# Weights and statistics of the next stage, loaded and made inside the scan loop

## The chip, the core and the metric

The kernel runs on one core of a Trainium2 chip. The time is that of the device for one execution of the whole program, in microseconds (us); of several executions the median is given. One more execution was recorded by the hardware profiler, and the views of the profile come from it. The engines are named as the profile names them: PE (matrix products) with PEld (its weight loads), DVE (VectorE), ACT (ScalarE), POOL (GpSimd) and SP (SyncE, which issues every DMA of this kernel).

## What is computed

The model has four layers over 4 images of 64 x 64 positions with 96 channels. Layers 0 and 1 are state-space blocks with a scan in four directions; layers 2 and 3 work on tokens and are not touched by the change. Of a scan layer, cut to what matters (layer 0; layer 1 is alike):

```python
x = x + _L0_conv_ref(_gn(x), ...)        # _gn: group normalisation over an image
xz = einsum('bhwc,ec->bhwe', x, in_proj_w)           # 96 -> 2 x 192
xx, z = split(xz, 2);  z = silu(z)
xc = silu(conv_3x3_depthwise(xx) + conv_b)
xs = [xc, xc transposed, xc reversed, xc transposed and reversed]   # K = 4 directions
dts, B, C = split(einsum('bkdl,kcd->bkcl', xs, x_proj_weight), [6, 22])
delta = softplus(einsum('bkrl,kdr->bkdl', dts, dt_projs_weight) + dt_projs_bias)
h = exp(delta * A) * h + delta * B * u      # for each of 4096 positions, 192 channels, 16 states
y = sum over states of h * C
y = layernorm(sum of the four directions) * ln_gamma + ln_beta
out = einsum('bhwe,ce->bhwc', y * z, out_proj_w)
```

The group normalisation needs the mean and the variance of every group over a whole image before the first product with `in_proj_w` can be right.

## The kernel before, in words

**Phases.** The two scan layers are worked in four phases: layer 0 for image pair 0, layer 0 for pair 1, layer 1 for pair 0, layer 1 for pair 1. `run` (L708) does, for each phase p, first the preparation of p with the finish of phase p-1 beside it, then the scan loop of p. After the last scan loop comes the finish of the last phase, and then the token layers.

**Preparation** (`prepare`, L151). It opens the pools `prep` and `steps`, loads the weights x_proj, dt_w, conv_b and Ds (L174), sums Ds (`dsum`, L182), and then makes the statistics of the two images: eight tiles `raw` of 96 x 8 x 2 x 64 numbers are loaded through two buffers (L190), and a bn_stats on DVE takes each half of each tile (L192). From these, for each of the two images, bn_aggr (L196), two small products with the group matrix (L198, L205) and an inverse root make `gs`, mean and scale of each channel. The loads of in_w and conv_w (L211, L174) follow. Then come the convolution (`convolve`, L231, which reads each image again in tiles `rawi`, L252, for the product L258) and the steps that make delta, delta times u, B and C and store them to DRAM (`steps`, L293).

**Finish** (`finish`, L555). It loads four weights, in_w (the half for z), out_w, gam and bet (L560 to L566), then for each quarter of the image loads `ud_f` and `yk` (L580, L590), undoes the directions on PE, and makes normalisation, gate, output product and residual. `run` advances it by one piece whenever the sum of `beside` over the preparation's pieces reaches 1. `beside` is 0 until the statistics and `gs` are made, so no piece of the finish is taken before that.

**Scan loop** (`scan_phase`, L478). It runs over 128 units: 8 chunks of 512 positions (NC), and in each 16 blocks (NEB) of 12 channels (EB). Its order is written out by hand (`manual_schedule`); outside the loop a scheduler orders the instructions of each engine. A unit `at` has 12 places n = 0 to 11. At each place PE replicates delta four places ahead (L424), ACT makes the decay three ahead (L428), DVE scans (L435), PE contracts the unit before (L453) and ACT evicts its result (L465); at every third place POOL multiplies h by B (L418), half a unit ahead. At n = 11 SP's work is issued in this order: the four y stores of the unit before (L473), the load of b for the next chunk after block 8 and of c after block 15 (L355), and the loads of unit at+3: dlt (L386) and six h loads (L408), two of 768 KB and four of 384 KB. The tiles: h has 4 buffers, dlt and d 3, the others 2. Every engine takes its instructions in the order of the program, SP too.

**DRAM layout of the input.** x and the result of the first layer lie as [pair, channel, 64, image, 64]. A `raw` tile of both images is therefore one run of 4096 bytes per channel; a tile of one image is 8 runs of 256 bytes.

Of the kernel before, what the change touches and what calls it, by code (L numbers as in the profile page):

```python
# [22 lines left out]
C = 96  # L23
E = 192
# [97 lines left out]
class Phase:  # L122


    def __init__(self, pre, pair, x_in, x_out):
        self.pre, self.pair, self.x_in, self.x_out = pre, pair, x_in, x_out

        self.beside = 0.0


class Scans:
    def __init__(self, tc, ctx, cst, a):
        nc = self.nc = tc.nc
        self.tc, self.cst, self.a = tc, cst, a

        def pool(name, bufs, **space):
            return ctx.enter_context(tc.tile_pool(name=name, bufs=bufs, **space))

        self.dram = pool("stage", 2, space=DRAM)
        self.keep = pool("keep", 2)  # L140
        cst.scans(tc, pool("const_s", 1))

    def bank(self):
# [7 lines left out]
    def prepare(self, ph):  # L151

        nc, cst, a, pre = self.nc, self.cst, self.a, ph.pre
        ph.gs = self.keep.tile([C, 2, 2], F32, name="gs", bufs=3)
        ph.delta = [
            self.dram.tile([G, NP16, E, TC], BF16, name="delta", bufs=2 * NC) for _ in range(NC)
        ]


        ph.du = [  # L160
            self.dram.tile([2, G, E + PITCH, TC], F32, name="du", bufs=2 * NC) for _ in range(NC)
        ]
        ph.bc = [self.dram.tile([NS // 2, G, 4, TC], F32, name="bc", bufs=2 * NC) for _ in range(NC)]
        ph.ud = self.dram.tile([C, 2, HW, 2, 64], F32, name="ud")
        ph.y = self.dram.tile([64, G, 2, 2, NEB, 16 * EB], F32, name="y")
        x = ph.x_in[ph.pair]

        with self.tc.tile_pool(name="prep", bufs=1) as wp, self.tc.tile_pool(
            name="steps", bufs=2
        ) as sp:  # L170

            def load(name, shape, at=0):
                t = wp.tile([at + shape[0]] + shape[1:], F32, name=name)
                nc.sync.dma_start(t[at:], a[pre + name])  # L174
                return t

            xp = load("x_proj", [C, 2, 2, XD2])
            dt_w = load("dt_w", [XD2 - 2 * NS, 2, E], at=2 * NS)
            conv_b = load("conv_b", [C, 2])
            ds = load("Ds", [C, 2, K])  # L180
            dsum = wp.tile([C, 2], F32, name="dsum")
            nc.vector.tensor_reduce(dsum, ds, mybir.AxisListType.X, ALU.add)  # L182
            yield


            st = wp.tile([C, 2, 8, 6], F32, name="st")
            with self.tc.tile_pool(name="stats", bufs=2) as rp:
                for hl in range(8):
                    raw = rp.tile([C, 8, 2, 64], F32, name="raw")
                    nc.sync.dma_start(raw, x[:, hl * 8 : hl * 8 + 8])  # L190
                    for i in range(2):
                        nc.vector.bn_stats(st[:, i, hl], raw[:, :, i])  # L192
                    yield
            for i in range(2):
                mv = wp.tile([C, 2], F32, name="mv")
                nc.vector.bn_aggr(mv, st[:, i].rearrange("p c s -> p (c s)"))  # L196
# [12 lines left out]
                yield  # L209
            in_w = wp.tile([C, E], F32, name="in_w")  # L210
            nc.sync.dma_start(in_w, a[pre + "in_proj_w"][:, :E])  # L211
            taps = load("conv_w", [C, 2, 9])

            xc = [wp.tile([C, 2, L], F32, name="xc", bufs=2) for _ in range(2)]
            ph.beside = 1.0
            yield
            yield from self.convolve(ph, 0, x, xc[0], in_w, taps, conv_b, dsum)
            ph.beside = 0.6
            other = self.convolve(ph, 1, x, xc[1], in_w, taps, conv_b, dsum)
            for i in range(2):  # L220
# [8 lines left out]
                ph.beside = 1.25  # L229

    def convolve(self, ph, i, x, xc, in_w, taps, conv_b, dsum):  # L231

# [242 lines left out]
                u.d[t::4, t].rearrange("p h l x -> p h (l x)"),  # L475
            )

    def scan_phase(self, ph):  # L478

# [16 lines left out]
        with self.tc.tile_pool(name="units", bufs=2) as self.units, self.tc.tile_pool(  # L496
            name="p_a", bufs=6, space=PSUM
        ) as self.p_a, self.tc.tile_pool(name="p_y", bufs=2, space=PSUM) as self.p_y:
            with self.tc.manual_schedule():
# [12 lines left out]
                    ahead(t, self.replicate)  # L512
                for t in range(LEAD - 1):
                    ahead(t, self.decay)
                for at, u in enumerate(units):
                    before = units[at - 1] if at else None
                    for n in range(EB):
                        t = at * EB + n
                        ahead(t + LEAD, self.replicate)
                        ahead(t + LEAD - 1, self.decay)  # L520
                        self.scan(u, n)
                        q, part = divmod(n, 3)
                        if before:
# [12 lines left out]
                        if n == 7 and u.eb >= NEB - 2 and u.c + 1 < NC:  # L536
                            self.weights(ph, u.c + 1, u.eb)
                        if n == EB - 1:
                            if before:
                                self.store(before)  # L540
                            if u.eb == 8 and u.c + 1 < NC:
                                self.load_b(ph, u.c + 1)
                            if u.eb == NEB - 1 and u.c + 2 < NC:
                                self.load_c(ph, u.c + 2)
                            if at + 3 < last:
                                self.load(units[at + 3])
# [8 lines left out]
    def finish(self, ph):  # L555
        nc, cst, a, pre = self.nc, self.cst, self.a, ph.pre
        x, x_out = ph.x_in[ph.pair], ph.x_out[ph.pair]
        with self.tc.tile_pool(name="fin", bufs=1) as fp:
            in_w = fp.tile([C, E], F32, name="in_w")
            nc.sync.dma_start(in_w, a[pre + "in_proj_w"][:, E:])  # L560
            out_w = fp.tile([C, 2, C], F32, name="out_w")
            nc.sync.dma_start(out_w, a[pre + "out_proj_w"])
            gam = fp.tile([128, E], F32, name="gam")
            nc.sync.dma_start(gam, a[pre + "gamma"].broadcast_to([128, E]))
            bet = fp.tile([128, E], F32, name="bet")
            nc.sync.dma_start(bet, a[pre + "beta"].broadcast_to([128, E]))  # L566
# [141 lines left out]
    def run(self, phases):  # L708


        for p in range(len(phases) + 1):
            with self.tc.tile_pool(name="p_c", bufs=2, space=PSUM) as self.p_c, self.tc.tile_pool(
                name="p_d", bufs=2, space=PSUM
# [9 lines left out]
                for _ in end:  # L723
                    pass
            if p < len(phases):
                self.scan_phase(phases[p])


@with_exitstack
# [268 lines left out]
```

## Time and profile before

| | |
|---|---|
| median of 3 runs | 11881.9 us (11853.94 to 11897.37) |
| the profiled execution | 11923.01 us, its span 11921.2 us |
| busy in the span | PE 72%, DVE 84%, ACT 62%, POOL 63% |
| chain that ended last | DMA 57%, PE 12%, DVE 11%, SP's queue 10% |
| DMA | 2501 MB, 210 GB/s over the span |
| mean granted PE clock | 0.827 |

By stages, cut at the first and last scan of each phase (busy us of the engines and GB/s of the DMA in the stage):

| stage | us | PE | DVE | ACT | POOL | GB/s |
|---|---|---|---|---|---|---|
| preparation 0 | 723.3 | 327.9 | 446.5 | 336.8 | 117.5 | 162 |
| scan loop 0 | 1870.7 | 1437.6 | 1806.5 | 1279.7 | 1741.9 | 250 |
| finish 0, preparation 1 | 847.2 | 538.0 | 551.2 | 431.7 | 122.9 | 183 |
| scan loop 1 | 1861.3 | 1434.2 | 1805.3 | 1276.4 | 1741.8 | 251 |
| finish 1, preparation 2 | 847.1 | 528.7 | 551.2 | 431.7 | 121.5 | 183 |
| scan loop 2 | 1860.3 | 1435.4 | 1805.0 | 1277.7 | 1742.9 | 251 |
| finish 2, preparation 3 | 850.8 | 540.8 | 551.2 | 432.1 | 120.9 | 182 |
| scan loop 3 | 1857.4 | 1436.1 | 1804.5 | 1276.5 | 1743.0 | 251 |
| finish 3 | 337.9 | 239.1 | 105.0 | 87.1 | 0.0 | 114 |
| token layers | 865.2 | 632.2 | 565.5 | 505.3 | 27.8 | 16 |

The shares over the span mix stages with different limits, so the stage is what to read. In a line of the profile that tells of a group of instructions, the text has the engine, the source line, the operation, and the tiles as out<-in with partitions x elements; after the bar or in brackets stands the idle time of that engine just before, and what ended it. "SPq" is SP's queue: an issue of a DMA, not the transfer.

### The profile page before, as it was taken

How to read it: one execution, taken by the hardware profiler on the slowest of the kernel's cores; microseconds unless marked ns; L12 is line 12 of the kernel's file. 1: busy time of each engine (PE TensorE's matmuls, PEld its weight loads, DVE VectorE, ACT ScalarE, POOL GpSimd, SP SyncE). 2: the span in 40 equal slices, each digit the busy share in tenths (PEclk: the TensorE clock that was granted, in tenths of full speed). 3: DMA queues.
4: the chain of work that ended last, by engine and by line, in shares of the span. 5: the costliest groups of instructions: out<-in, count | busy, mean ns of one | idle time of the engine just before them, and what ended most of it. 6: DMA issues, size and time to landing. Idle time of an engine off the chain costs nothing.

```text
span 11921.2 us, 337611 instructions
## 1 busy us (share of the span) xinstructions
PE 8549.8 (72%) x144992; PEld 4586.7 (38%) x144992; DVE 9991.8 (84%) x10247; ACT 7335.1 (62%) x12106; POOL 7480.2 (63%) x2316
## 2 busy tenths in 40 slices
PE   4557777765767777765767777766667777777777
PEld 1124444432334444442334444433234444444333
DVE  6679999977779999987769999986769999993667
ACT  4556666655556666655556666655557666662556
POOL 0169999961159999970149999980149999980000
PEclk8578999986679999986679999887578898998887
DMA  3677777765677777765777777765677777763110
GB/s 99 192 244 250 253 255 254 251 208 144 201 241 256 253 253 251 253 217 146 204 229 258 256 253 251 253 217 149 198 226 255 255 255 253 253 229 124 18 22 11
DMA packets 952266, 2501.22 MB, mean 210 GB/s; under 512 B 324494, under 2 KB 607220, under 8 KB 819316
## 3 DMA queue, kind: packets, MB, share of 16 engines
q1 hardware_dynamic: 950772, 2479.63, 63.0%
q8 instruction: 1142, 18.71, 0.7%
q14 instruction: 352, 2.88, 0.1%
HBM read 1965.42 MB, written 513.80 MB: 208 GB/s over the span
## 4 chain that ended last, share of the span: by engine, by line
DMA 57%; PE 12%; DVE 11%; SPq 10%; ACT 5%; issue 3%; POOL 2%; POOLq 0%; DVEq 0%; ACTq 0%
DMA h<-du 53%; SPq L408 9%; DVE xc L277 4%; PE f L603 2%; POOL parts L331 2%; PE d L317 1%; DVE dl L328 1%; PE f L683 1%; PE c L300 1%; DVE du_sb L327 1%; PE f L694 1%; DVE parts L332 1%; DMA yk<-y 1%; PE f L669 1%; PE f L612 1%
## 5 line engine op out<-in xcount | busy, mean ns | idle before, releaser
L418 POOL TENSOR_TENSOR h<-h,b 128x1536 f32<-128x1536 f32 x2048 | 7020.9, 3461 | 574.0 <-DMA h<-du 229.6
L435 DVE TENSOR_TENSOR_SCAN h<-a,carry,h 128x512 f32<-128x512 f32 x5376 | 6353.3, 1259 | 202.8 <-POOL h L418 199.4
L428 ACT ACTIVATE a<-a,a_col 128x512 f32<-128x512 f32 x6144 | 4038.5, 664 | 1888.6 <-PE a L424 1852.8
L453 PEld LDWEIGHTS y<-h,cw 128*32 128x32 f32 x131072 | 2785.0, 128 | 3534.2 <-issue 1369.4
L453 PE MATMUL y<-h,cw 128*32 128x48 f32 x131072 | 3658.4, 266 | 522.4 <-DVE h L435 205.3
L424 PE MATMUL a<-dlt,rep 72*128 72x512 bf16 x6144 | 2534.2, 422 | 1352.5 <-DVE h L435 1254.1
L331 POOL CAST parts<-dl 96x1024 bf16<-96x1024 f32 x256 | 431.2, 1688 | 2687.6 <-DVE dl L328 1979.4
L465 ACT COPY d<-y 128x384 f32<-128x384 f32 x2048 | 979.7, 478 | 467.7 <-PE y L453 414.9
L435 DVE TENSOR_TENSOR_SCAN h<-a,h 128x512 f32<-128x512 f32 x768 | 868.2, 1200 | 179.7 <-ACT a L428 113.4
L277 DVE SCALAR_TENSOR_TENSOR xc<-xp,conv_w,xc 96x512 f32<-96x512 f32 x1024 | 716.3, 760 | 154.2 <-ACT xc L275 110.0
L424 PEld LDWEIGHTS <-rep 72*128 72x128 bf16 x6144 | 487.5, 98 | 849.3 <-issue 613.9
L317 PE MATMUL d<-xd,dt_w 7*96 7x512 f32 x1024 | 532.0, 885 | 263.6 <-ACT dl L325 141.2
L835 POOL MEMSET tn<- 1x4096 f32 x8 | 27.8, 3506 | 861.5 <-PE pa L855 515.4
L300 PE MATMUL c<-xc,x_proj 96*103 96x512 f32 x512 | 442.0, 1002 | 115.7 <-ACT xp L261 54.6
L327 DVE TENSOR_TENSOR du_sb<-dl,xc 96x1024 f32<-96x1024 f32 x256 | 409.9, 1607 | 123.6 <-ACT dl L325 67.2
L603 PE MATMUL f<-yk,perm 128*128 128x384 f32 x1024 | 415.6, 549 | 106.4 <-DMA yk<-y 81.0
L325 ACT ACTIVATE dl<-d 96x1024 f32<-96x1024 f32 x256 | 257.7, 1018 | 348.6 <-DVE parts L332 259.2
L328 DVE TENSOR_TENSOR dl<-dl,parts 96x1024 f32<-96x1024 f32 x256 | 309.8, 1216 | 190.7 <-ACT parts L326 187.8
L332 DVE TENSOR_TENSOR parts<-dl,parts 96x1024 bf16<-96x1024 f32 x256 | 326.2, 1280 | 170.0 <-POOL parts L331 168.8
L317 PEld LDWEIGHTS d<-xd,dt_w 7*96 7x96 f32 x1024 | 160.0, 216 | 586.5 <-ACT xd L303 200.1
L258 PE MATMUL c<-rawi,in_ws 96*96 96x512 f32 x256 | 195.5, 874 | 241.3 <-ACT xp L261 101.6
L370 ACT ACTIVATE cw<-c,gmask 128x256 f32<-128x256 f32 x512 | 285.5, 569 | 129.3 <-DMA dlt<-delta 66.7
(119 smaller groups left out, 5764.0 us busy)
## 6 DMA issues: line engine op xcount, KB each, us to landing
h<-du SPq DMA_DIRECT2D x1024, 768.0 KB
h<-du SPq DMA_DIRECT2D x2048, 384.0 KB
du<-du_sb SPq DMA_DIRECT2D x512, 384.0 KB
delta<-parts SPq DMA_DIRECT2D x256, 576.0 KB
dlt<-delta SPq DMA_DIRECT2D x512, 288.0 KB
y<-d SPq DMA_DIRECT2D x2048, 48.0 KB
yk<-y SPq DMA_DIRECT2D x256, 384.0 KB
ud<-xu SPq DMA_DIRECT2D x128, 192.0 KB
```

The source lines that it names most:

```text
L277: nc.vector.scalar_tensor_tensor(rows(acc), src, w, rows(acc), ALU.mult, ALU.add)
L300: nc.tensor.matmul(rows(ps[:XD2]), xp[:, k, h], u[:, h], start=h == 0, stop=h == 1)
L317: nc.tensor.matmul(ps[:, m], dt_w[part, k, m * C : (m + 1) * C], xd[part], start=True, stop=True)
L331: nc.gpsimd.tensor_copy(parts[:, 1], delta)
L408: self.nc.sync.dma_start(u.h[32 * first : 32 * (first + quarters), e : e + n].rearrange("p e t -> p (e t)"), source.rearrange("a g e t -> ...
L418: self.nc.gpsimd.tensor_tensor(h, h, b, ALU.mult)
L424: self.nc.tensor.matmul(u.a[n], self.cst.rep[:, h], u.dl[:, e], start=True, stop=True)
L428: self.nc.scalar.activation(u.a[n], u.a[n], AF.Exp, scale=u.ph.a_col[:, at : at + 1])
L435: self.nc.vector.tensor_tensor_scan(u.h[:, n], u.a.pop(n), u.h[:, n], 0.0 if u.c == 0 else u.ph.carry[:, at : at + 1], ALU.mult, ALU.add,)
L453: self.nc.tensor.matmul(view(u.y[32 * j : 32 * j + 32], l2 * EB, (8 * EB, 4), (1, EB)), u.ph.cw[u.c][:, l1, 8 * j + l2], view(u.h, 64 * l1 ...
L465: self.nc.scalar.copy(u.d[:, :, :, l1], u.y[:, : 32 * EB].rearrange("p (t h x) -> p t h x", t=4, h=2))
L603: nc.tensor.matmul(ps[:, : 4 * C].rearrange("p (w v e) -> p w v e", w=4, v=nv), cst.perm[:, k], view(t, off, (sw if k < 2 else -sw, 4), (1 ...
```

## The change

A new pool `weights` holds the ten weights of finish and preparation, one buffer each. A phase's preparation no longer loads its six weights; `prepare_weights` makes a list of six small tasks of it. For phase 0 `run` calls them at the start. The finish no longer loads its four; `finish_weights` makes four tasks of it. `statistics` makes 17 tasks: task n reduces tile n-1 and loads tile n, a tile now being one image's 96 x 8 x 64 numbers (16 tiles of 192 KB instead of 8 of 384 KB). In the scan loop, from unit 32 on, place 8 of each unit takes the next task of the list: the four weights of this phase's finish, then the six of the next preparation, then the 17 of its statistics, 27 in all (4 in the last loop). The loop's `raw` tile has the two buffers of the loop's pool. The preparation of phase 0 has no loop before it and runs the 17 tasks itself.

```diff
@@ prepare
-            xp = load("x_proj", [C, 2, 2, XD2])
-            dt_w = load("dt_w", [XD2 - 2 * NS, 2, E], at=2 * NS)
-            conv_b = load("conv_b", [C, 2])
-            ds = load("Ds", [C, 2, K])
+            xp, dt_w, conv_b, ds, in_w, taps = ph.prep_w
...
-            st = wp.tile([C, 2, 8, 6], F32, name="st")
-            with self.tc.tile_pool(name="stats", bufs=2) as rp:
-                for hl in range(8):
-                    raw = rp.tile([C, 8, 2, 64], F32, name="raw")
-                    nc.sync.dma_start(raw, x[:, hl * 8 : hl * 8 + 8])
-                    for i in range(2):
-                        nc.vector.bn_stats(st[:, i, hl], raw[:, :, i])
-                    yield
+            if ph.st is None:
+                with self.tc.tile_pool(name="stats", bufs=2) as rp:
+                    for part in self.statistics(ph, rp):
+                        part()
+                        yield
+            st = ph.st
...
-            in_w = wp.tile([C, E], F32, name="in_w")
-            nc.sync.dma_start(in_w, a[pre + "in_proj_w"][:, :E])
-            taps = load("conv_w", [C, 2, 9])
@@ new
+    def weight(self, name, shape, source, at=0):
+        t = self.wts.tile([at + shape[0]] + shape[1:], F32, name=name)
+        self.nc.sync.dma_start(t[at:], source)
+        return t
...
+    def prepare_weights(self, ph):
...
+        return [
+            lambda: load("x_proj", [C, 2, 2, XD2]),
+            lambda: load("dt_w", [XD2 - 2 * NS, 2, E], 2 * NS),
+            lambda: load("conv_b", [C, 2]),
+            lambda: load("Ds", [C, 2, K]),
+            load_in,
+            lambda: load("conv_w", [C, 2, 9]),
+        ]
...
+    def statistics(self, ph, pool):
...
+        ph.st = self.keep.tile([C, 2, 8, 6], F32, name="st")
...
+            raw = pool.tile([C, 8, 64], F32, name="raw")
+            nc.sync.dma_start(raw, x[:, hl * 8 : hl * 8 + 8, i])
...
+            nc.vector.bn_stats(ph.st[:, i, hl], loaded.pop(0).rearrange("c a p -> c (a p)"))
...
+            def part(n=n):
+                if n:
+                    reduce(*at[n - 1])
+                if n < len(at):
+                    load(*at[n])
@@ scan_phase(self, ph, after)
+                side = self.finish_weights(ph)
+                if after:
+                    side += self.prepare_weights(after)
+                    side += self.statistics(after, self.units)
+                side = iter(side)
...
+                        if n == 8 and at >= 2 * NEB:
+                            part = next(side, None)
+                            if part:
+                                part()
@@ finish
-            in_w = fp.tile([C, E], F32, name="in_w")
-            nc.sync.dma_start(in_w, a[pre + "in_proj_w"][:, E:])
...
+            in_w, out_w, gam, bet = ph.fin_w
@@ run
+        for part in self.prepare_weights(phases[0]):
+            part()
...
-                self.scan_phase(phases[p])
+                self.scan_phase(phases[p], phases[p + 1] if p + 1 < len(phases) else None)
```

More of the change, by code (lines that the diff above doesn't have):

```diff
@@ L128, in __init__ @@
         self.beside = 0.0
+        self.st = None
 class Scans:
@@ L140, in __init__ @@
         self.keep = pool("keep", 2)
+        self.wts = pool("weights", 1)
         cst.scans(tc, pool("const_s", 1))
@@ L170, in prepare @@
         ) as sp:
[L172 to L175, printed above, removed]
-            xp = load("x_proj", [C, 2, 2, XD2])
-            dt_w = load("dt_w", [XD2 - 2 * NS, 2, E], at=2 * NS)
-            conv_b = load("conv_b", [C, 2])
-            ds = load("Ds", [C, 2, K])
+            xp, dt_w, conv_b, ds, in_w, taps = ph.prep_w
             dsum = wp.tile([C, 2], F32, name="dsum")
@@ L229, in prepare, with load, load_in, finish_weights @@
                 ph.beside = 1.25
+    def weight(self, name, shape, source, at=0):
[3 more added lines that the diff above has]
+    def prepare_weights(self, ph):
+        def load(name, shape, at=0):
+            ph.prep_w.append(self.weight(name, shape, self.a[ph.pre + name], at))
+        def load_in():
+            ph.prep_w.append(self.weight("in_w", [C, E], self.a[ph.pre + "in_proj_w"][:, :E]))
+        ph.prep_w = []
+        return [
[6 more added lines that the diff above has]
+        ]
+    def finish_weights(self, ph):
+        a, pre = self.a, ph.pre
+        ph.fin_w = []
+        return [
+            lambda: ph.fin_w.append(self.weight("z_w", [C, E], a[pre + "in_proj_w"][:, E:])),
+            lambda: ph.fin_w.append(self.weight("out_w", [C, 2, C], a[pre + "out_proj_w"])),
+            lambda: ph.fin_w.append(
+                self.weight("gam", [128, E], a[pre + "gamma"].broadcast_to([128, E]))
+            ),
+            lambda: ph.fin_w.append(
+                self.weight("bet", [128, E], a[pre + "beta"].broadcast_to([128, E]))
+            ),
+        ]
+    def statistics(self, ph, pool):
+        nc, x = self.nc, ph.x_in[ph.pair]
+        ph.st = self.keep.tile([C, 2, 8, 6], F32, name="st")
+        loaded = []
+        def load(hl, i):
+            raw = pool.tile([C, 8, 64], F32, name="raw")
+            nc.sync.dma_start(raw, x[:, hl * 8 : hl * 8 + 8, i])
+            loaded.append(raw)
+        def reduce(hl, i):
+            nc.vector.bn_stats(ph.st[:, i, hl], loaded.pop(0).rearrange("c a p -> c (a p)"))
+        at = [(hl, i) for hl in range(8) for i in range(2)]
+        for n in range(len(at) + 1):
+            def part(n=n):
[3 more added lines that the diff above has]
+                    load(*at[n])
+            yield part
     def convolve(self, ph, i, x, xc, in_w, taps, conv_b, dsum):
@@ L476, in store, with scan_phase @@
             )
-    def scan_phase(self, ph):
+    def scan_phase(self, ph, after):
         nc = self.nc
@@ L558, in finish @@
         with self.tc.tile_pool(name="fin", bufs=1) as fp:
-            in_w = fp.tile([C, E], F32, name="in_w")
-            nc.sync.dma_start(in_w, a[pre + "in_proj_w"][:, E:])
[L561 to L566, printed above, removed]
+            in_w, out_w, gam, bet = ph.fin_w
             for q in range(4):
```

## The prediction

> **What bounds the kernel now.** I read the busy times in ten windows first, cut at the first and last scan (L435) of each phase. The four scan loops take 1870.7, 1861.3, 1860.3 and 1857.4 us, the preparations between them 847 to 851. A border has two edges, so both were looked at.
>
> In the loop VectorE is busy 97% of the time and GpSimd 93%, but neither sets the pace. The timelines of the two engines (start, length, line; in brackets the idle time before it) and then the chain of waits:
>
> ```profile
> 1217.40 14.21 DVE L435 TENSOR_TENSOR_SCAN h<-a,carry,h 128x512 f32<-128x512 f32 x12 [0.91 <-POOL h L418]
> 1232.47 14.21 DVE L435 TENSOR_TENSOR_SCAN h<-a,carry,h 128x512 f32<-128x512 f32 x12 [0.86 <-POOL h L418]
> ...
> 1213.92 13.69 POOL L418 TENSOR_TENSOR h<-h,b 128x1536 f32<-128x1536 f32 x4 [1.41 <-DMA h<-du]
> ```
>
> ```profile
> 1511.69 12.98 DMA h<-du
> 1524.68 0.02 issue
> 1524.69 0.69 SPq L408
> ```
>
> A unit is 12 scans, 14.2 us of VectorE and 13.7 us of GpSimd, yet units come every 14.6 us (scan start to scan start, mean after the eighth unit). VectorE waits 0.46 to 0.51 us at its first scan for GpSimd, and GpSimd 0.9 us at its first product for the DMA. The chain then stays in one loop: an h load lands, SP issues the next, that one lands. SP's issues use eight completion semaphores in turn, so an issue waits for the DMA eight places before it. The transfers set the pace, and VectorE has about 0.4 us a unit to spare.
>
> The DMA packet records say what saturates. For 97% of a scan loop at least 8 packets are in work on the 16 engines, for 27% exactly 8. An h load of 768 KB makes 16 semaphore updates, one of 384 KB makes 9, of which the first comes at once: the four small ones of each unit run on 8 engines. Those eight are nearly full, the other eight are not.
>
> At the border to the second phase (timeline):
>
> ```profile
> 2604.64 0.35 SPq L174 DMA_DIRECT2D x_proj<-in_L_x_proj  x1
> 2605.05 0.27 SPq L174 DMA_DIRECT2D dt_w<-in_L_dt_w  x1
> ...
> 2613.64 0.16 DVE L182 TENSOR_REDUCE dsum<-Ds 96x2 f32<-96x8 f32 x1 [19.50 <-DMA Ds<-in_L_Ds]
> 2613.86 2.47 DVE L192 BATCH_NORM_STATS2 st<-raw 96x6 f32<-96x512 f32 x4
> ...
> 2631.46 0.35 DVE L196 BATCH_NORM_AGGREGATE mv<-st 96x2 f32<-96x48 f32 x1
> ...
> 2640.98 3.73 PE L258 MATMUL c<-rawi,in_ws 96*96 96x512 f32 x4 [1.83 <-DVE ln L118]
> ```
>
> The last scan ended at 2594.0. SP waits until 2604.6 for the landing of the last y store, only then loads weights, and eight raw tiles go through two buffers. Nothing else runs: the convolution needs the statistics, and the finish begins beside it.
>
> **Gain at the borders.** From that first load (x_proj) to the first bn_aggr: 2604.64 to 2631.46, 5313.34 to 5340.84, 8020.57 to 8047.42: 26.8, 27.5 and 26.85 us. All of it goes, except the wait on the same landing and dsum, about 0.5 us: 26.3 + 27.0 + 26.35 = **79.7 us**. What is late next is the chain from bn_aggr to L258, 9.5 us, unchanged. L258's first two tiles are already there: of the 32 rawi loads (L252) of a phase, the first phase's stretch holds 34, the last two at 375.6 and 377.3 us. The finish's ud_f and yk loads, issued in 1.8 + 5.2 us, can start at 2604.7 and are in before the PE gets to them some 12 us later; without that cover a wait of up to 5 us a border appears. The last finish loses its four weight issues, 10728.84 to 10730.92: **2.1 us**.
>
> **Loss in the first phase.** It has no loop before it, so it still makes its statistics, now with 16 loads of 192 KB and one reduction behind each, where there were 8 of 384 KB. The nearest row is the rawi load, same shape: issued 41.84, used by the PE at 44.55, so 2.7 us. Two buffers then give two loads per 2.7 + 0.7 + 0.1 = 3.5 us; 14 after the first pair are 24.5 us, ending near 39 where it now ends at 31.7: **-7.5 us** (5 to 13).
>
> **Cost in the loop.** Per phase 0 to 2: 4 weights of the finish in units 32 to 35, 6 of the preparation in 36 to 41, 16 raw loads in 42 to 57 and 16 reductions in 43 to 58. Each is one more issue on SP (0.3 to 0.4 us), one more place in the ring of eight, and packets on the full engines.
>
> VectorE: a bn_stats is 0.67 us, issue to issue 0.61. A unit then needs at least 14.1 + 0.68 = 14.8 us against 14.6, so at least 0.2 us a unit if nothing else changes.
>
> The wait for raw: in program order it stands behind the h loads of the unit before and ahead of the y stores. SP gets there about 2 us into the next unit. The y stores issued there land 12.9 to 14.0 us into it (semaphore records, three units), so raw lands near 14. The reduction stands behind scan 8 of that unit, which ends at 10.66. VectorE stops there for about 3.4 us, with three scans of this unit and all of the next queued behind, and PE and ScalarE with them. I take that as paid once, not sixteen times: VectorE then runs 3.5 us later against a DMA stream that doesn't wait for it, and raw lands as VectorE arrives. How far it may lag is seen in one unit: its last eviction (L465) ended at 1522.94, its y store was issued at 1527.58, so 4.6 us. After unit 58 the 0.5 us that VectorE waits per unit pays the lag back in some 8 units.
>
> What is not paid back is time of the full engines. The nearest rows: rawi's 768 packets of 256 B occupied all 16 engines 1.04 to 1.29 us, so 1.0 to 1.1 us an engine. The trace holds a trial of an added load: b and c (256 KB, 128 packets), one each per 16 units between the y stores and dlt. Folding the issue times of dlt over units 16 to 111 of all phases: 14.6 in a usual unit, 16.16 then 13.11 around c, 16.82 then 12.87 around b. The pairs exceed 29.2 by 0.07 and 0.49 us. So one more load and one more place in the ring cost 0.1 to 0.5 us. Sixteen in a row can't use a neighbour's slack: from below 0.2 (VectorE's floor), from above 1.1 (every packet). I take about 1.0 less the 3% of idle time (0.44 us), 0.55: 16 x 0.55 = **8.8 us a phase** (3 to 18).
>
> The weights: nine are 0.1 to 0.6 us an engine, inside the idle share, 0.3 us together. dt_w is different. By its bytes, 106 KB at the loop's 250 GB/s, it costs 0.4 us. In the trace its 71 packets went out from 2606.28 to 2612.30, 6.0 us, while the loads around it had finished on 15 engines by 2611.8 and got their last update at 2613 to 2615. The Trainium skill (DMA: Bandwidth & Descriptors, "Why a DMA increments its semaphore by 16 and not by 1") says that the number of engines is the largest one up to 16 that divides the slowest dimension of both sides, and that these are the lowest-numbered. 71 is prime, so one engine, and that one is among the eight that the 384 KB loads (slowest dimension 8) use. It speaks against moving this load into the loop. By the bytes the phase costs 9.5 us, by the rule up to 15; I take the rule's side, 5 us after some idle time: **14 us a phase**, 42 in three. Which engine a packet ran on isn't in the records.
>
> **Sum.** 79.7 + 2.1 - 7.5 - 42 = 32 us faster. The profiled execution took 11,923.0 (span 11,921.2 and 1.8 around it), so 11,891 there. It lay 41 us above the median of three, 11,881.9; from the median, **11,850 us**. Those three spread 43 us; below 0.5% (59 us) I count as no change.
>
> **Rivals.**
> 1. The loop takes it all in: VectorE's floor and nothing more, about 3 us a phase. For it: b and c cost next to nothing. Against: each of these has two light units behind it. 79.7 + 2.1 - 7.5 - 9 = 65 faster, 11,817.
> 2. Slower: the stop for raw recurs in every unit. Place: the reduction behind scan 8. Price: 3.4 us x 16 x 3 = 163, with 3 x 5 for dt_w. It decides once VectorE's lag passes the 4.6 us: then the y stores wait for the evictions, the h loads and the next raw behind them move back too, and lag makes lag. Against: the first stop and the reduction make 4.1 us. 163 + 15 - 74 = 104 slower, 11,986.
> 3. The border gives less: the finish's yk loads, which now meet the last y store, or another order of the preparation's instructions keep 10 us of each 26. Against: nothing in the preparation but the statistics waited there. 32 - 30 = 2 faster, 11,880.
>
> **How the numbers follow.** Forecast 0.53 (its bounds: loop cost 5 to 25 a phase, 11,817 to 11,883), rival 1 0.20, rival 2 0.12, rival 3 0.15. Rival 1 is faster by over 0.5% in most of its cases and the forecast in a few: 0.23. Slower is rival 2 and a tail of 3: 0.15. The rest, 0.62, is within 0.5%. The range leaves out most of rival 2 and a tail below: 11,795 to 11,925; the likeliest case alone is 11,815 to 11,885.
>
> **What would show it.** Right: bn_aggr about 11 us after the last scan of a phase in place of 37; the first convolution of phase 0 some 8 us later; in units 43 to 58 a VectorE wait for raw at L192 of about 3 us once and under 1 us after, units of 15.0 to 15.4 us, and a unit of some 19 near unit 38 to 40 (dt_w); the later units back to 14.1 until the lag is gone. Wrong: L192 waiting 3 us in unit after unit, or loops lengthened by over 25 us; or loops unchanged within 5.

## The result, and the profile after

| | before | after |
|---|---|---|
| median | 11888.89 us (12 runs, 11853.94 to 11907.95) | 11862.08 us (12 runs, 11829.40 to 11886.42) |
| ratio | | 0.9975 [0.9964, 0.9986] |
| the profiled execution | 11923.01 us, span 11921.2 | 11847.12 us, span 11845.3 |

The change makes the kernel 26.8 us faster (0.25%, by the interval 17 to 43 us), where 32 were forecast. Measured once more beside later runs it was 0.9968 [0.9955, 0.9980], 43 us (24 to 54) faster.

The spans differ by 76 us, three times as much as the medians. The profiled execution of before took longer than all of its 12 timed runs and that of after less than its median. A single pair of profiles therefore can't be subtracted; the sums below use the stages of several. Where a gain or a loss is given in us, it is the difference of the medians, and the figures in brackets are the 95% interval of the ratio, turned into us.

**The border.** Timeline of the kernel after at the border to the second phase, first DVE, then PE, then SP's queue (start, duration, line, operation; in brackets the idle time before it and what ended it). The last scan ended at 2590.4.

```profile
2601.09 0.16 DVE L176 TENSOR_REDUCE dsum<-Ds 96x2 f32<-96x8 f32 x1 [10.51 <-DMA y<-d]
2601.16 0.36 DVE L188 BATCH_NORM_AGGREGATE mv<-st 96x2 f32<-96x48 f32 x1
...
2607.28 0.32 DVE L289 TENSOR_SCALAR in_ws<-in_w,gs 96x192 f32<-96x192 f32 x1
...
2637.84 1.53 DVE L328 SCALAR_TENSOR_TENSOR xc<-xp,conv_w,xc 96x512 f32<-96x512 f32 x2 [16.70 <-ACT xc L326]
```

```profile
2609.80 6.83 PE L656 MATMUL f<-yk,perm 128*128 128x384 f32 x12 [0.94 <-DMA yk<-y]
2618.49 0.89 PE L656 MATMUL f<-yk,perm 128*128 128x384 f32 x2 [1.86 <-DMA yk<-y]
...
2620.75 1.02 PE L309 MATMUL c<-rawi,in_ws 96*96 96x512 f32 x2
```

```profile
2601.10 1.75 SPq L633 DMA_DIRECT2D ud_f<-ud  x4
2602.88 6.45 SPq L643 DMA_DIRECT2D yk<-y  x8
2609.38 1.67 SPq L303 DMA_DIRECT2D rawi<-in_x  x2
```

The first bn_aggr comes 10.7 us after the last scan (11.0 and 10.9 at the other borders), where it came 37.5, 38.3 and 37.5 us after it. The weight loads and the reductions are gone. But the product for the convolution (now L309) starts 19.6 us behind bn_aggr (17.0 and 18.0 at the other borders); it was 9.5. Its first two tiles used to stand ahead of the finish's yk product on PE (L603 before, now L656). The scheduler now puts L656 in front of them, and L656 waits for yk, which SP issues only from 2602.88 on. DVE's first convolution is 47.4 us behind the last scan instead of 70.8: 23.4 us gained of the 26.7 that bn_aggr gained. At the other two borders it is 26.1 of 27.3 and 24.1 of 26.6.

**The loop.** DVE's timeline of the kernel after at the first raw tile, in unit 43 of the first loop:

```profile
1342.78 10.68 DVE L486 TENSOR_TENSOR_SCAN h<-a,carry,h 128x512 f32<-128x512 f32 x9 [0.27 <-POOL h L469]
1356.15 0.69 DVE L269 BATCH_NORM_STATS2 st<-raw 96x6 f32<-96x512 f32 x1 [2.69 <-DMA raw<-in_x]
1356.76 14.19 DVE L486 TENSOR_TENSOR_SCAN h<-a,carry,h 128x512 f32<-128x512 f32 x12
1371.26 0.69 DVE L269 BATCH_NORM_STATS2 st<-raw 96x6 f32<-96x512 f32 x1 [0.31 <-DMA raw<-in_x]
1371.87 14.19 DVE L486 TENSOR_TENSOR_SCAN h<-a,carry,h 128x512 f32<-128x512 f32 x12
1385.98 0.67 DVE L269 BATCH_NORM_STATS2 st<-raw 96x6 f32<-96x512 f32 x1
...
1431.47 0.69 DVE L269 BATCH_NORM_STATS2 st<-raw 96x6 f32<-96x512 f32 x1 [1.33 <-DMA raw<-in_x]
...
1552.95 0.69 DVE L269 BATCH_NORM_STATS2 st<-raw 96x6 f32<-96x512 f32 x1 [1.70 <-DMA raw<-in_x]
```

The one long stop is the first, 2.69 us (3.45 and 3.37 in the other loops), then 0.31, then nothing for three reductions. Shorter waits for raw come back later: the 15 behind the first add up to 5.2 us in this loop (4.0 and 5.6 in the others), nine of them are under 0.15 us and the longest is 1.70. The gaps between scans are gone in these units: between two reductions stand 12 scans in 14.19 us. Behind the last reduction, still in the first loop:

```profile
1582.57 0.69 DVE L269 BATCH_NORM_STATS2 st<-raw 96x6 f32<-96x512 f32 x1
1583.18 131.00 DVE L486 TENSOR_TENSOR_SCAN h<-a,carry,h 128x512 f32<-128x512 f32 x111
1715.49 4.81 DVE L486 TENSOR_TENSOR_SCAN h<-a,carry,h 128x512 f32<-128x512 f32 x4 [1.31 <-POOL h L469]
```

111 scans, more than nine units, run without a gap at 14.2 us a unit. Against the usual 14.6 that gives some 4 us back, in about the number of units that was forecast. In the other loops of the two profiles of this kernel the waits return after three to fourteen units.

### The profile page after: what moved, and what is told of

Its sections match the earlier page's. It is cut to its first block, busy times and chain, and to the rows that moved or that the text cites. A ratio compares the mean times of both kernels' runs of the same rounds, so it can differ in the third digit from the quotient of the medians.

```text
span 11845.3 us, 337639 instructions
## 1 busy us (share of the span) xinstructions
PE 8552.8 (72%) x144992; PEld 4590.0 (39%) x144992; DVE 9985.8 (84%) x10247; ACT 7329.0 (62%) x12106; POOL 7486.5 (63%) x2316
## 4 chain that ended last, share of the span: by engine, by line
DMA 56%; PE 12%; DVE 12%; SPq 10%; ACT 5%; issue 3%; POOL 2%; DVEq 0%; POOLq 0%; ACTq 0%
DMA h<-du 48%; SPq L459 8%; DVE xc L328 4%; PE f L656 2%; DMA raw<-x 2%; POOL parts L382 2%; DVE h L486 1%; PE f L736 1%; DVE dl L379 1%; DMA raw<-in_x 1%; PE d L368 1%; DVE du_sb L378 1%; DMA yk<-y 1%; DVE parts L383 1%; PE f L747 1%
## 5 line engine op out<-in xcount | busy, mean ns | idle before, releaser
L656 PE MATMUL f<-yk,perm 128*128 128x384 f32 x1024 | 419.7, 554 | 105.6 <-DMA yk<-y 103.9
L309 PE MATMUL c<-rawi,in_ws 96*96 96x512 f32 x256 | 191.6, 855 | 237.7 <-ACT xp L312 110.0
```

The source lines that it names most:

```text
L656: nc.tensor.matmul(ps[:, : 4 * C].rearrange("p (w v e) -> p w v e", w=4, v=nv), cst.perm[:, k], view(t, off, (sw if k < 2 else -sw, 4), (1 ...
```

## The experiments

There were twelve runs of eleven kernels, the kernel after among them. "Slower" and "faster" below are against the kernel before in the same batch, with the 95% interval.

**1 and 2: the statistics' work in the loop alone.** 16 loads and 16 reductions are added to the kernel before, in units 42 to 58, then in units 111 to 127. The borders stay as they were. `side` holds 17 tasks like those of the change's `statistics`, on tiles of their own; the second kernel has `at >= 111`.

```diff
@@ scan_phase of before, place 8
+                        if n == 8 and at >= 42:
+                            part = next(side, None)
+                            if part:
+                                part()
```

> The kernel before, with 16 raw loads of 192 KB and 16 reductions added in units 42 to 58 of the first three scan loops; their results are not used and the borders stay as before. The forecast (16 x 0.55 us of the full DMA engines a phase, not won back): 26 us slower than before, 9 to 54. The rival (VectorE only falls behind and wins it back in later units, at 0.4 to 0.5 us a unit): 0 to 9 slower, with units 42 to 58 some 9 to 12 us longer a phase and units 59 to 127 as much shorter.

> The same 16 loads and reductions, but in units 111 to 127, at the end of the loop, where no unit is left to win anything back. The forecast, a price paid in DMA time: as the run in units 42 to 58, 26 us slower than before. The rival, a lag that is won back: 27 to 36 slower (9 to 12 a phase), against 0 to 9 for the same work in units 42 to 58.

Measured: no difference (14 us faster to 10 slower) in units 42 to 58; 15 us slower (2 faster to 24 slower) in units 111 to 127. The first excludes most of what the forecast allowed (9 to 54) and fits the lag that is won back. The second lies below both expectations; the two intervals overlap, so a difference by place is not shown by the times. The scan starts in the traces do point to it. In the mean of three loops, units 43 to 58 of the first kernel take 15.04 us against 14.68 in the profile of before, and units 59 to 75 take 14.38 against 14.61: 5.7 us a phase are lost and 3.8 come back. In the second kernel units 112 to 126 take 15.0 against 14.6, and no unit is left to win it back.

**3 and 4: the two halves of the change.** First the weights come in the loop and the statistics stay at the border; then the other way round.

```diff
@@ weights alone: scan_phase of after
-                    side += self.statistics(after, self.units)
@@ statistics alone: scan_phase of after (weights loaded in prepare and finish, as before)
-                side = self.finish_weights(ph)
+                side = iter(())
...
-                    side += self.prepare_weights(after)
-                    side += self.statistics(after, self.units)
-                side = iter(side)
+                    side = self.statistics(after, self.units)
...
-                        if n == 8 and at >= 2 * NEB:
+                        if n == 8 and at >= 42:
```

> The kernel after, but the statistics are made at the border from eight 384 KB loads, as before; only the ten weights of a phase come in the loop. By the forecast's terms: each border wins the 9.2 us from the x_proj load to the first reduction, less 0.5, so 26 us in three, and 2 at the last finish; the loop pays 5.3 us a phase, 16, nearly all of it dt_w: 12 faster than before. If the loop takes the weights in for nothing: 28 faster.

> The kernel before, but the statistics of the next pair are loaded and reduced in units 42 to 58 of the loop and used at the border; the weights are loaded at the border as before, and the first phase makes its statistics from 16 loads. By the forecast's terms: each border wins the 17.6 us from the first reduction to the first bn_aggr, 53 in three, the first phase loses 7.5 and the loops 26: 19 faster than before. If the loop and the first phase lose nothing: 53 faster.

Measured: weights alone 4 us slower (6 faster to 19 slower), so there is no gain; statistics alone 70 us faster (57 to 98). With the weights alone the borders do get shorter, 839.0 us in the mean where those of the unchanged kernels have 843.5, with the first convolution 63.4 to 64.9 us behind the last scan instead of some 70. The four loops of that one profile are 17 us longer than those of before, which would take it back; but loops scatter as much. SP's queue and DVE of the kernel with the statistics alone, at the same border (last scan ended at 2594.6), show why the weights bring so little once the statistics are gone:

```profile
2605.20 0.35 SPq L176 DMA_DIRECT2D x_proj<-in_L_x_proj  x1
...
2607.47 0.43 SPq L211 DMA_DIRECT2D in_w<-in_L_in_proj_w  x1
```

```profile
2605.19 0.37 DVE L196 BATCH_NORM_AGGREGATE mv<-st 96x2 f32<-96x48 f32 x1 [10.44 <-DMA y<-d]
...
2615.01 0.31 DVE L300 TENSOR_SCALAR in_ws<-in_w,gs 96x192 f32<-96x192 f32 x1
...
2642.44 7.68 DVE L339 SCALAR_TENSOR_TENSOR xc<-xp,conv_w,xc 96x512 f32<-96x512 f32 x11 [11.20 <-ACT xc L337]
```

The weights are issued at the moment bn_aggr runs and travel beside the normalisation chain. in_ws is 20.4 us behind the last scan, against 16.9 in the kernel after. At the first convolution some 2 of these 3.6 us are left: over the six borders of two profiles each it comes 48.0 us behind the last scan with the statistics alone, 45.9 in the kernel after.

**5 to 7: is the difference between "after" and "statistics alone" real, and is dt_w its cause?** Both again in one batch, with the kernel after whose dt_w comes as 64 and 7 rows.

```diff
@@ prepare_weights of after
-            lambda: load("dt_w", [XD2 - 2 * NS, 2, E], 2 * NS),
+            load_dt,
@@ load_dt
+            self.nc.sync.dma_start(t[2 * NS : 2 * NS + 64], src[:64])
+            self.nc.sync.dma_start(t[2 * NS + 64 :], src[64:])
```

> The kernel after, once more, beside the runs that follow. Theory A (the ten weights in the loop cost what the statistics alone don't pay): 27 us faster than before, as at first, and some 40 slower than the kernel with the statistics alone. Theory B (the two were only measured at different times; the weights in the loop cost nothing and win nothing): as the kernel with the statistics alone, the two within 10 us.

> The kernel with the statistics alone in the loop, once more. Theory A: 70 us faster than before, as at first. Theory B: within 10 us of the kernel after, somewhere between 27 and 70 faster than before.

> The kernel after, with dt_w loaded as 64 and 7 rows in place of 71 rows at once. If the 71-row load costs the loop 5 us a phase, as forecast: some 15 us faster than the kernel after; if it is the whole of 14 us a phase by which theory A has the weights cost: 43 faster. If it is priced by its bytes (0.4 us a phase): no difference, within 3.

Measured: after 43 us faster (24 to 54), statistics alone 72 faster (51 to 81), after with the split dt_w 39 faster (30 to 58). The statistics alone win in both batches; here the medians are 11843.2 and 11871.6 us. Theory A holds. The split changes nothing that can be seen, so the form of the dt_w load is not what the weights cost.

**8: dt_w in the loop, multiplied.** The 71-row load in every eighth unit of the kernel before, 56 times.

```diff
@@ scan_phase of before, place 8
+                        if n == 8 and at % 8 == 2 and 8 <= at < 122:
+                            t = self.units.tile([XD2 - 2 * NS, 2, E], F32, name="dt_again")
+                            nc.sync.dma_start(t, self.a[ph.pre + "dt_w"])
```

> The kernel before, with the 71-row dt_w load repeated in every eighth unit from 10 to 114 (14 times in each of the four loops, 56 in all), its data not used. At 5 us each, as forecast: 280 us slower than before. By its bytes, 0.4 us each: 22 slower. By unit 39 of the profile of the kernel after (16.1 to 16.9 us against a usual 14.6): 2 us each, 110 slower, less what later units win back.

Measured: 53 us **faster** (37 to 68). No theory had that sign. DVE's timeline of this kernel, from unit 91 on:

```profile
2043.33 28.31 DVE L435 TENSOR_TENSOR_SCAN h<-a,carry,h 128x512 f32<-128x512 f32 x24 [0.16 <-POOL h L418]
2076.08 112.98 DVE L435 TENSOR_TENSOR_SCAN h<-a,carry,h 128x512 f32<-128x512 f32 x96 [4.45 <-POOL h L418]
2192.32 112.91 DVE L435 TENSOR_TENSOR_SCAN h<-a,carry,h 128x512 f32<-128x512 f32 x96 [3.26 <-POOL h L418]
```

Two units behind each load DVE stops, here 4.45 and then 3.26 us. Between the stops 96 scans, eight units, run without a gap. By the trace's records a unit with the stop takes 16.1 to 17.6 us in the mean of the four loops, the seven others mostly 14.1 to 14.5. Eight units of before take 8 x 14.62 = 117.0 us, here, with 14.53 in the mean of all four loops, 116.3. One stop costs less than the small waits that it replaces. Over the 56 loads that is some 38 us, most of the 53.

**9: one load and one reduction in every unit**, 112 a loop in three loops: the tasks of experiment 1, seven times over.

```diff
@@ scan_phase of before, place 8
+                        if n == 8 and at >= 8:
```

> The kernel before, with a 192 KB raw load and a reduction in every unit from 8 to 120 of the first three loops (112 of each a loop), results not used. The forecast's price (0.55 us of DMA time each): 185 us slower than before. The rival, VectorE as the bound (14.1 + 0.61 to 0.68 us a unit against the usual 14.6): 25 to 70 slower, with units of 14.7 to 14.8 and hardly a wait. If raw's landing stops VectorE time and again (1 us and more a unit): over 300 slower.

Measured: 71 us slower (56 to 91), 0.21 us for a load with its reduction. DVE's timeline:

```profile
1451.86 0.69 DVE L243 BATCH_NORM_STATS2 st_again<-raw_again 96x6 f32<-96x512 f32 x1 [1.30 <-DMA raw_again<-in_x]
1452.47 14.19 DVE L460 TENSOR_TENSOR_SCAN h<-a,carry,h 128x512 f32<-128x512 f32 x12
1466.58 0.67 DVE L243 BATCH_NORM_STATS2 st_again<-raw_again 96x6 f32<-96x512 f32 x1
```

The shortest units are 14.69 us (14.1 and a reduction), the mean 14.8 to 14.9. DVE is the bound in the shortest units, and stops for raw come on top of it; 0.55 us of DMA time for each is refuted.

**10: a stop without a DMA.** Four reductions of a resident tile in every eighth unit.

```diff
@@ scan_phase of before, place 8, every eighth unit
+                            if at == 10:
+                                still = self.units.tile([C, TC], F32, name="still", bufs=1)
+                                nc.sync.dma_start(still.rearrange("c (a p) -> c a p", p=64), ph.x_in[ph.pair][:, 0:8, 0])
...
+                            for j in range(4):
+                                nc.vector.bn_stats(st[:, j], still)
```

> The kernel before, with four reductions of a resident tile (2.5 us of VectorE) in every eighth unit of each loop, 56 in all, and no DMA with them. If a stop of VectorE is what lets the DMA stream get ahead, so that the seven units behind it run without a wait: 20 to 60 us faster than before, as with the dt_w loads. If it is the added load that does it (its place in the ring, or the pause it makes on SP): no gain, 0 to 140 slower (56 x 2.5 us if nothing is hidden, near 0 if the usual waits of 0.5 us a unit take it in).

Measured: 21 us faster by the medians, but no clear difference (27 faster to 8 slower), although 56 x 2.4 = 134 us of DVE work were added. DVE's timeline shows two things, one at unit 10 and one later:

```profile
859.64 10.29 DVE L435 TENSOR_TENSOR_SCAN h<-a,h 128x512 f32<-128x512 f32 x9 [1.29 <-POOL h L418]
888.53 2.47 DVE L544 BATCH_NORM_STATS2 st_still<-still 96x6 f32<-96x512 f32 x4 [18.60 <-DMA still<-in_x]
...
1460.62 2.44 DVE L544 BATCH_NORM_STATS2 st_still<-still 96x6 f32<-96x512 f32 x4
1462.99 112.89 DVE L435 TENSOR_TENSOR_SCAN h<-a,carry,h 128x512 f32<-128x512 f32 x96
1575.80 2.44 DVE L544 BATCH_NORM_STATS2 st_still<-still 96x6 f32<-96x512 f32 x4
```

The tile is loaded and used in one task, with no unit between: DVE stood 18.6 us. By the records this happens once a loop, 17.9 us in the mean, 72 us in all. The five units behind it belong to the first chunk, where a scan is shorter; they take 13.4 us each, in before 14.5, which gives 5.8 us back each time.

What follows differs from loop to loop. In loops 0 and 2 the lines above stand for all: behind every later pause 96 scans, eight units, run without a gap, and up to the last eight units a unit takes 14.40 us, where units of before take 14.6. In loops 1 and 3 it is 14.52 and 14.57, and the small waits come back before the next pause. DVE in loop 1:

```profile
4274.54 2.44 DVE L544 BATCH_NORM_STATS2 st_still<-still 96x6 f32<-96x512 f32 x4
4276.90 74.20 DVE L435 TENSOR_TENSOR_SCAN h<-a,carry,h 128x512 f32<-128x512 f32 x63
4351.76 14.21 DVE L435 TENSOR_TENSOR_SCAN h<-a,carry,h 128x512 f32<-128x512 f32 x12 [0.66 <-POOL h L418]
```

SP's longest waits over seven and eight units show the difference (total us, times, longest), first in loop 0 (1462 to 1560), then in loop 1 (4263 to 4380):

```profile
SPq L473 <- ACT a L428: 29.9, 5, 7.3
SPq L408 <- DMA h<-du: 6.2, 5, 2.0
```

```profile
SPq L408 <- DMA h<-du: 36.0, 23, 2.9
```

In loop 0 SP stands mostly at the y stores (L473), waiting for ScalarE's results, so the transfers are ahead and wait for the computing engines. In loop 1 it stands at the h loads (L408), waiting for earlier transfers, as in the kernel before. Right behind the long stop SP issues dlt 1.2 to 1.4 us into a unit in all four loops, against 6.9 in the mean of before. In loops 0 and 2 that lead lasts to the end or nearly so, in loops 1 and 3 it is gone within some twenty units. So a loop whose transfers are ahead runs without waits, and no load in every eighth unit is needed for it. But whether the pauses of 2.4 us bring the lead about, or only keep for a while what the stop of 18 us gave, this kernel can't tell.

**11: dt_w in every eighth unit as 64 and 7 rows.**

```diff
-                            nc.sync.dma_start(t, self.a[ph.pre + "dt_w"])
+                            nc.sync.dma_start(t[:64], self.a[ph.pre + "dt_w"][:64])
+                            nc.sync.dma_start(t[64:], self.a[ph.pre + "dt_w"][64:])
```

> The kernel before, with the dt_w load of every eighth unit as 64 and 7 rows in place of 71 at once. If the gain of 53 us with the 71-row load comes from its long stop (3 us at the unit two behind it, then seven units of 14.1): the stop is under 1 us here and the gain is gone, within 15 us of before. If any added place in the ring does it: some 50 us faster, as there.

Measured: 36 us slower (20 to 51), and no unit with a stop: in the mean of the four loops every unit from 16 on lies between 14.2 and 15.5. DVE's timeline in the stretch that was shown for the 71-row load:

```profile
2076.34 14.21 DVE L435 TENSOR_TENSOR_SCAN h<-a,carry,h 128x512 f32<-128x512 f32 x12 [0.84 <-POOL h L418]
2090.92 14.21 DVE L435 TENSOR_TENSOR_SCAN h<-a,carry,h 128x512 f32<-128x512 f32 x12 [0.37 <-POOL h L418]
2105.88 14.21 DVE L435 TENSOR_TENSOR_SCAN h<-a,carry,h 128x512 f32<-128x512 f32 x12 [0.75 <-POOL h L418]
```

The small waits are back in every unit of this stretch. The 53 us went with the stop. What remains is the price of two more loads, 36 / 112 = 0.32 us each (0.18 to 0.46).

**12: both gains together.** The statistics alone and the 71-row load in every eighth unit.

> The kernel with the statistics alone in the loop and the 71-row dt_w load in every eighth unit of each loop as well, its data not used. If the two gains lie in different places (borders, loops) they add: 125 us faster than before (72 and 53), 100 to 145. If the statistics' own stop in the loop already does what the load does: 75 to 95 faster.

Measured: 71 us faster (54 to 88), the same as the statistics alone. The gains don't add. Its records show the stops again, with most units between them at 14.1 to 14.6, and its four loops are 16 us shorter together than in the two profiles of the statistics alone. But the first convolution comes 52 to 56 us behind the last scan, where it was 48 without the load, and the three borders are 13 us longer together. Why the borders change isn't shown.

## Why the forecast came right, step by step

Mean stage lengths in us, with the number of stages. "As before" takes the borders of seven kernels that leave them alone, and the seven loops to which nothing was added; "after" two profiles of the kernel after, "statistics alone" two of that kernel.

| stage | as before | after | statistics alone |
|---|---|---|---|
| preparation 0 | 720.8 (7) | 723.3 (2) | 720.3 (2) |
| a border | 843.5 (21) | 819.6 (6) | 821.3 (6) |
| a scan loop | 1860.2 (7) | 1867.1 (8) | 1863.7 (8) |
| last finish and token layers | 1204.2 (7) | 1211.9 (2) | 1206.4 (2) |

For the kernel after that is 3 x -23.9 + 4 x 6.9 + 2.5 + 7.7 = -34 us; its two medians were -27 and -43. The loops are the uncertain term: those of the kernel after range from 1855.4 to 1888.6 us, those of before from 1853.4 to 1870.7. Four of the seven loops as before are last loops, which are short (1857.2 in the mean). Compared place by place, the loops of the kernel after are 7.7, 12.0 and 1.0 us longer and 1.7 shorter, 19 in place of 28, and the sum is -43; but each of the first three places then rests on a single profile of before.

- **The gain at the borders, 79.7 forecast: 72.** bn_aggr moved by what was said. The step that fell short is the next one, the chain from bn_aggr to the convolution's product "unchanged", with yk in time. The order on PE changed and the product waits behind yk: 7.5 to 10 us more there, 1 to 3 us at the first convolution. That is rival 3's mechanism at a third of its size or less.
- **Whose gain it is.** The forecast's stretch from the x_proj load to bn_aggr gave the weights 9.2 us of it. A border of the statistics alone is as short within 2 us. The loads of the weights were on the path only because the raw loads stood behind them; with these gone, the normalisation chain covers all but some 2 us of them. The sum was nearly right for both edits together. For the weights alone it was too high: bn_aggr came 5 us earlier with them, not 9.
- **The first phase, 7.5 lost: 0 to 2.5.** The reductions end at 39.4 us, as worked out (39), and the first convolution comes 4.2 us later. The stage doesn't get longer by it: what stands behind took it in. The seven kernels with borders as before scatter from 718.2 to 723.3 us there, as much as what is left.
- **The stop for raw: right in the main.** One long stop, 2.4 to 3.5 us in six loops (3.4 forecast); of the 90 later waits 7 are over 1 us, which was to be the limit. Units 43 to 58 take 15.1 to 15.3 us in the mean, then 14.1 until the lag is gone. Rival 2 did not come: the lag stayed inside its slack, and in experiment 9 even 112 tasks in a row didn't make it grow.
- **16 raw loads, 8.8 us a phase: none of it in experiment 1, at most 3 (10 / 3 by its interval).** The row it was taken from (b and c, 0.1 to 0.5 us) was the better price than the packets' 1.1 us; experiment 9 has 0.21. The step that failed is "what is not paid back is time of the full engines". Loops 0 and 2 of experiment 10 made their transfers at 14.40 us a unit for a hundred units, and SP even had to wait for results, so the engines were not full at 14.6.
- **dt_w, 5 us a phase: a stop of 2 to 3 us, and no loss that can be seen.** Unit 39 took 16.1 to 16.9 us in one profile and 16.4 to 18.0 in the other, not 19; with the split load it took 14.1 to 15.0, and the kernel was no faster for it. The rule that was weighed (the Trainium skill, DMA: Bandwidth & Descriptors, "Why a DMA increments its semaphore by 16 and not by 1") agrees with experiments 8 and 11 in so far as the regular stop is there with 71 rows and gone with 64 and 7; that it is one engine's work fits the border's semaphore records (its load makes 2 updates, a 384 KB load makes 9), but no record names the engine. But the price drawn from the rule was wrong, and for the load in every eighth unit even in sign: a stop in this loop is not a loss by its length.
- **The last finish, 2.1 gained: nothing, and 8 us lost.** The finish starts 2 us earlier and ends where it did. Behind it lies a term that the forecast didn't have, the token layers, which no line of the diff touches. The timeline of all engines before and then after, around the last addition of the finish (xo):

```profile
11055.21 0.69 DVE L696 TENSOR_TENSOR xo<-f,xs 96x512 f32<-96x512 f32 x1 [1.58 <-PE f L694]
...
11063.50 0.64 SPq L887 DMA_DIRECT2D t<-x  x1
...
11076.07 1.99 PE L784 MATMUL pa<-t,mean_c 96*96 96x512 f32 x2 [20.89 <-DMA raw<-in_L_ffn_W]
```

```profile
10969.50 0.69 DVE L749 TENSOR_TENSOR xo<-f,xs 96x512 f32<-96x512 f32 x1 [2.98 <-PE f L747]
...
10984.78 9.61 SPq L942 DMA_DIRECT2D t<-x  x2
...
10999.18 1.99 PE L839 MATMUL pa<-t,mean_c 96*96 96x512 f32 x2 [29.72 <-issue]
```

  The first load of the tokens (t) is issued 7 us later against xo, now behind the last feed-forward weights, and the first product comes 29 us behind xo instead of 20. All four profiles of kernels with the pool `weights` have t at 14.5 to 14.9 us behind xo and the first product at 25.8 to 29.0; the ten without it have 7.3 to 7.7 and 18.7 to 20.3. From xo to the end it is 868.5 to 875.1 us in the four and 861.7 to 865.4 in the ten. That the pool moves the tokens' tiles or the scheduler's order is the likely reason, but neither was changed by itself.

So the total was right in part by luck, because errors cancelled: 8 too much at the borders and 10 missing at the last finish and the token layers, against 14 to 23 too much in the loops and 5 to 7 in the first phase. A different split of the 27 us within the noise of the loops is possible. One bound of the forecast was also worked out wrongly: 11,817 us belongs to a loop cost of 3 us a phase, and 5 us give 11,823.

**What stays open.** The kernel after took 28 us more than the one with the statistics alone in the batch that had both. The last stage is 5 to 6 of it, the first 3; four loops at 3.4 us are 14, and they scatter too much to name an instruction. The borders go the other way by 5, so the profiles account for 17. And why the ordinary loop falls into small waits, when a stop leaves it free of them for several units, wasn't settled. SP's issue of dlt came 6.9 us into a unit of before in the mean, and 5.0 to 6.6 us into the units between two stops of experiment 8, so the stream is further ahead there; what takes that lead away, within twenty units in two loops of experiment 10 and not in the two others, is not shown. A short pause of DVE whose tile is loaded early, alone or with the statistics, wasn't tried.

**The better version.** The kernel with the statistics alone in the loop beats both: 0.9935 [0.9918, 0.9952] and 0.9945 [0.9932, 0.9957] of the time before, with less code than the change. The weights are better left at the border.

## What to carry to other kernels

Price edits that lie on one path together and singly: once the longest of them is gone, the others may be covered anyway, and what they cost elsewhere (here some 28 us) is then nearly all that they bring. In a loop with little slack, a wait's length is not its price: look at the units behind it, which can win back all of it or more, and look at every loop before you say so, because one and the same loop can run ahead of its transfers or behind them. And when a scheduler orders the code between hand-ordered parts, take its new order, on every engine and also in stages that the diff doesn't touch, as a term of the sum.

## What the runs showed of the hardware that was not expected

The same loop ran in two ways. With its transfers ahead (dlt issued some 1 us into a unit) two loops of experiment 10 took 14.40 us a unit, a pause of 2.4 us of VectorE in every eighth unit included; with its transfers behind (6.9 us into a unit) the loop of before took 14.6 without any pause. All four loops of experiment 10 were ahead after a stop of 16.5 to 18.6 us, and two fell back. A 192 KB load that was used in the task that issued it cost those 16.5 to 18.6 us of VectorE, against 2.4 to 3.5 us for the first load with one unit between and mostly under 1 us for the following ones. Executions of one and the same program, taken in two batches, differ in a single loop by up to 20 us (1868.1 and 1888.6 for the first loop of the kernel after) at a granted clock of 0.825 over the whole run in both, which is why a gain of 5 us a stage needs several profiles.
